# Two-layer cross attention on one core: bias sums added by GpSimd instead of by transfers, and the last layer's vectors loaded later

## The chip, the cores and the metric

The kernel runs on one core of a Trainium2 chip, in fp32 throughout. The metric is the time of one execution on the device, in microseconds (us). The time given for a kernel is the median of its runs; the profile is one further execution.

## What is computed

There are two cross-attention layers over the same context. B = 8 batches of T = 100 query rows of width E = 1024, and per batch S = 1444 context rows of width L = 512.

```python
# layer 0: x is (8, 100, 1024), ctx is (8, 1444, 512)
Q = x @ Wq + bq;  K = ctx @ Wk + bk;  V = ctx @ Wv + bv
w = softmax(Q @ K.T / sqrt(1024), axis=-1)        # over the context rows
x = x + (w @ V) @ Wo + bo
# layer 1: its own weights, the same ctx
q = x @ Wq1 + bq1;  k = ctx @ Wk1 + bk1;  v = ctx @ Wv1 + bv1
w = softmax(q @ k.T / sqrt(1024), axis=1)         # over the query rows
y = w @ v + x
out = (y - mean(y)) * rsqrt(var(y) + 1e-6) * gamma + beta     # mean and variance over the last axis
```

## The kernel before

**Stages.** The kernel never forms keys and values. It first multiplies weights with weights: `qk0` (Wq Wkᵀ of layer 0), then `vo0` (Wv Wo), then, after layer 0's queries, `qk1` (Wq1 Wk1ᵀ). Each of these `weight_products` (L350) is a product in Strassen-Winograd form: seven half-sized products x, z, w, y and so on, issued by `half_steps` (matmul in L166), with the sums of blocks between them on VectorE. Queries then meet the context directly: `scores_by_keys` (matmul in L957) makes the scores of one batch out of `cT` tiles (the context, transposed), and `weighted_rows` (matmul in L910) weighs the `c` tiles (the context as it is) with them. `alternated` interleaves the two: the weighing of batch b with the scores of batch b+2. Then come the output projection of layer 0, the queries of layer 1, and layer 1's attention for the batches 0 to 3, 4 to 6 and 7, with a projection behind each set. `finish` (`untransposed` and `normalise`) ends a batch of layer 1 some batches later; `project_last` ends batch 7.

**Sums for the biases.** A bias turns into weighted sums over the rows of weights, eight scaled 128x1024 rows for each. `transferred_sum` (L549) makes such a sum without VectorE: `scaled_sum` (L580) lets ScalarE write eight scaled copies (L583) and then adds them pairwise, as a tree of seven additions. Each addition is `transfer_added` (L577): a DMA issued by GpSimd from SBUF to SBUF that accumulates into its destination. `key_bias_sums` (L628) does the same for three of the eight terms of `kb0` (128x800 each), and leaves five to VectorE. For `qk1` the tree covers all eight rows (`acc_c`), and for the narrower `acc_u` it adds 128x512 rows.

**Buffers.** Streamed data lies in a pool `stream` of ten "unit" buffers (`unit`); three more buffers of the tag `prob` (`feature_block`) hold `cT` tiles, and in the weight products the scaled rows of the sums. Each batch of each layer loads four `c` tiles, two `cT` tiles into units and two into `prob` buffers, 5.9 MB in all. A `cT` tile is loaded in two parts (L867), in the kernel before as in the changed one.

**Order.** TensorE's order is written out by hand. The loads are issued by SyncE (SP) in a fixed order (`loaded_in_order`, L859, issue in L860), VectorE has stretches in program order (`vector.in_order`), and ScalarE's scaling is in program order; the rest is placed by the scheduler. GpSimd also issues all DMAs of `nc.gpsimd.dma_start`.

**Vectors and output.** After the queries of layer 1 (L1378 to L1388) two units are taken for `vectors` and kept until the end: they hold `gamma`, `beta` and the two halves of `bv1`, each broadcast to 128 partitions. Then `out[0]` to `out[6]` are set to `beta` by seven DMAs of 400 KB from SBUF (L1386), since `normalise` ends with a DMA that accumulates the scaled rows into `out[b]` (L1244). Last, `wv1` is loaded (L1388). `vectors` are first read by `untransposed(0)` in batch 4 of layer 1 (L1229).

## Time and profile before

| | |
|---|---|
| runs, us | 592.06, 594.5, 2132.2 (median 594.5) |
| profiled execution, us | 591.46 |
| its span, us | 589.7 (1.8 us lie around it) |
| TensorE clock granted | 0.996 |
| PE (TensorE matmul) busy, us | 574.6 (97%), 7470 instructions |
| DVE (VectorE) busy, us | 399.9 (68%) |
| POOL (GpSimd) busy, us | 134.7 (23%) |
| ACT (ScalarE) busy, us | 133.2 (23%) |
| DMA | 142.95 MB, mean 242 GB/s; queue q1 (loads) 56.5%, q0 (issued by GpSimd) 19.0% of 16 engines |

How to read the views: the page gives busy times by engine and, in 40 slices of 14.7 us each, the busy share of each engine and of the DMA engines in tenths. The chain is the work that ended last, followed back through what released it. The waits list for each engine and line what it waited for: us in total, times, longest. A table of windows gives for each stretch of time the busy time of PE, PEld (weight load), DVE, ACT and POOL with the count of instructions, the clock, the DMA share (1.00 is all 16 engines busy) and GB/s.

### The profile page before, as it was taken

How to read it: one execution, taken by the hardware profiler on the slowest of the kernel's cores; microseconds unless marked ns; L12 is line 12 of the kernel's file. 1: busy time of each engine (PE TensorE's matmuls, PEld its weight loads, DVE VectorE, ACT ScalarE, POOL GpSimd, SP SyncE). 2: the span in 40 equal slices, each digit the busy share in tenths (PEclk: the TensorE clock that was granted, in tenths of full speed). 3: DMA queues.
4: the chain of work that ended last, by engine and by line, in shares of the span. 5: the costliest groups of instructions: out<-in, count | busy, mean ns of one | idle time of the engine just before them, and what ended most of it. 6: DMA issues, size and time to landing. Idle time of an engine off the chain costs nothing.

```text
span 589.7 us, 17503 instructions
## 1 busy us (share of the span) xinstructions
PE 574.6 (97%) x7470; PEld 496.8 (84%) x7470; DVE 399.9 (68%) x936; ACT 133.2 (23%) x349; POOL 134.7 (23%) x206
## 2 busy tenths in 40 slices
PE   9999999999999999999999999999989999999994
PEld 8887457678899999999998666788989999999992
DVE  1997589879676973956658696957334446754695
ACT  1331421523510112221101001103233302153313
POOL 3110110221211222441123002206622112341052
PEclk9999999999999999999999999999999999999998
DMA  8959989944699999999953507629999991699114
GB/s 277 311 126 319 305 223 285 254 84 100 111 278 344 372 366 363 370 373 359 333 194 100 203 0 300 196 69 375 375 309 316 352 364 46 180 319 281 53 30 83
DMA packets 65096, 142.95 MB, mean 242 GB/s; under 512 B 7548, under 2 KB 12924, under 8 KB 65020
## 3 DMA queue, kind: packets, MB, share of 16 engines
q1 hardware_dynamic: 56574, 117.80, 56.5%
q0 software_dynamic: 8048, 23.57, 19.0%
q8 instruction: 59, 0.97, 0.7%
q10 hardware_dynamic: 398, 0.47, 0.2%
q14 instruction: 17, 0.14, 0.1%
HBM read 121.53 MB, written 6.14 MB: 217 GB/s over the span
## 4 chain that ended last, share of the span: by engine, by line
PE 94%; issue 2%; POOL 1%; DVE 1%; ACT 1%; DVEq 0%; POOLq 0%
PE s L957 22%; PE A L910 21%; PE qk_x L166 7%; PE g_x L166 5%; PE o_x L166 5%; PE vo_x L166 4%; PE o_y L166 3%; PE g_y L166 3%; PE qk_y L166 2%; PE qk_z L166 2%; PE o_z L166 1%; PE o_w L166 1%; PE qk_w L166 1%; PE vo_y L166 1%; PE vo_z L166 1%
## 5 line engine op out<-in xcount | busy, mean ns | idle before, releaser
L910 PE MATMUL A<-w,c 128*64 128x100 f32 (+1 forms) x3072 | 228.5, 249 | 2.7 <-issue 2.7
L910 PEld LDWEIGHTS A<-w,c 128*64 128x64 f32 (+1 forms) x3072 | 202.5, 137 | 3.8 <-issue 3.5
L957 PE MATMUL s<-g1T,cT 128*64 128x100 f32 (+1 forms) x1472 | 114.8, 249 | 3.4 <-issue 3.4
L957 PE MATMUL s<-g0T,cT 128*64 128x100 f32 (+1 forms) x1472 | 112.2, 249 | 0.3 <-issue 0.2
L957 PEld LDWEIGHTS s<-g1T,cT 128*64 128x64 f32 (+1 forms) x1472 | 99.8, 136 | 5.9 <-issue 5.3
L957 PEld LDWEIGHTS s<-g0T,cT 128*64 128x64 f32 (+1 forms) x1472 | 98.8, 136 | 2.9 <-DMA c<-in_ctx 1.3
L1169 POOL TENSOR_TENSOR part<-w 128x500 f32<-128x500 f32 x16 | 26.5, 1655 | 122.5 <-ACT w L1017 58.2
L1149 ACT ACTIVATE w<-w,negmax 128x100 f32<-128x100 f32 x96 | 35.0, 367 | 72.8 <-DVE negmax L99 72.8
L99 DVE SCALAR_TENSOR_TENSOR w<-s,kb 128x400 f32<-128x400 f32 (+2 forms) x32 | 13.9, 464 | 41.1 <-PE s L957 40.9
L1017 ACT ACTIVATE w<-w 128x400 f32<-128x400 f32 (+2 forms) x32 | 12.0, 443 | 120.5 <-DVE w L99 120.5
L99 DVE TENSOR_REDUCE most<-s 128x100 f32<-128x400 f32 (+1 forms) x24 | 12.5, 521 | 36.6 <-PE s L957 36.5
L166 PE MATMUL qk_x<-qk 128*128 128x256 f32 x128 | 29.9, 382 | 0.0
L166 PEld LDWEIGHTS qk_x<-qk 128*128 128x128 f32 x128 | 23.6, 192 | 3.0 <-ACT qk L440 0.2
L1229 DVE SCALAR_TENSOR_TENSOR z<-vectors,r,z 100x512 f32<-100x512 f32 x16 | 11.4, 744 | 12.9 <-PE z L1227 12.8
L99 DVE TENSOR_TENSOR w<-w,rtotal 128x400 f32<-128x400 f32 (+2 forms) x32 | 18.3, 571 | 1.1
L969 POOL MEMSET w<- 68x100 f32 x16 | 3.8, 238 | 64.0 <-PE A L910 46.0
L1242 ACT ACTIVATE z<-z,rstd 100x1024 f32<-100x1024 f32 x7 | 8.0, 1150 | 45.4 <-POOL rstd L1240 45.4
L1149 ACT ACTIVATION_READ_ACCUMULATOR w<-w,negmax 128x1 f32 x96 | 18.1, 188 | 0.0
L99 DVE TENSOR_TENSOR xT<-xT,o_x 128x400 f32<-128x400 f32 (+1 forms) x32 | 15.9, 540 | 2.7 <-PE o_x L166 2.4
L578 POOL DMA_DIRECT2D qk_L_xattn_bk<-qk_L_xattn_bk x6 | 5.2, 922 | 47.3 <-DMA qk_L_xattn_bk<-qk_L_xattn_bk 19.0
L673 ACT ACTIVATE g1T<-g_x,k 128x400 f32<-128x400 f32 x4 | 2.4, 594 | 59.4 <-PE g_x L166 59.3
L166 PE MATMUL vo_x<-vo 128*128 128x512 f32 x32 | 15.3, 595 | 0.0
(435 smaller groups left out, 1052.9 us busy)
## 6 DMA issues: line engine op xcount, KB each, us to landing
c<-in_ctx SPq DMA_DIRECT2D x176, 256.0 KB, 6.1
cT<-in_ctxT SPq DMA_DIRECT2D x64, 370.0 KB, 6.8
cT<-in_ctxT SPq DMA_DIRECT2D x64, 352.0 KB, 5.9
vo<-in_L_xattn_Wo SPq DMA_DIRECT2D x8, 512.0 KB, 7.4
qk<-in_L_xattn_WqT SPq DMA_DIRECT2D x8, 512.0 KB, 6.0
qk<-in_L_xattn_WqT SPq DMA_DIRECT2D x15, 256.0 KB, 4.9
xT<-in_xT SPq DMA_DIRECT2D x2, 1600.0 KB, 24.6
qk_L_xattn_bk<-qk_L_xattn_bk POOLq DMA_DIRECT2D x6, 512.0 KB, 8.5
```

Source lines behind the costliest of these rows:

```text
L99: ins = getattr(nc.vector, op)(*args, **kw)
L166: nc.tensor.matmul(banks[n // per][:, n % per * width : (n % per + 1) * width], lhs[i][:, n * P : (n + 1) * P], rhs[i], start=(fresh and i ...
L578: nc.gpsimd.dma_start(out=to, in_=t, accum_op=ALU.add)
L673: nc.scalar.activation(dst[g][:, c, :], banks[j][:, :GT], AF.Identity, bias=u[:, c : c + 1])
L910: nc.tensor.matmul(ps[h * HP : (h + 1) * HP, k * T : (k + 1) * T], c[m // CQ][:r, m % CQ, k * P + h * HP : k * P + (h + 1) * HP], w[:r, m, :],
L957: nc.tensor.matmul(to, cT[k][:, o : o + n], q[:, k, t0 : t0 + T], start=(k == 0 and m % GM == 0), stop=(k == LC - 1 or (k == LC - 2 and no ...
L969: nc.gpsimd.memset(s["w"][:PAD, MC - 1, :], 0.0)
L1017: nc.scalar.activation(rows, rows, AF.Exp)
L1149: nc.scalar.activation(rows[:, i, :], rows[:, i, :], AF.Exp, bias=negmax[:, i : i + 1], accum_out=total[:, i : i + 1])
L1169: add(part, w[:, 0:5, :], w[:, 5:10, :], ALU.add)
L1229: nc.vector.scalar_tensor_tensor(z[:, half], bv1[j][:T], s["r"], ps[:T, :], ALU.mult, ALU.add)
L1242: nc.scalar.activation(z, z, AF.Copy, scale=rstd)
```

## The change

Two sums no longer use transfers: the seven additions of `acc_c` in `qk1` and the three of `kb0` become `tensor_tensor` instructions of GpSimd (128x1024 and 128x800). The sums of `qk0`, `vo0` and the additions of `acc_u` stay as they are. The two `vectors` units are allocated and loaded behind layer 1's fourth batch (b == 3) instead of ahead of its first. The seven DMAs that set `out[b]` to `beta` no longer read the SBUF tile, but read `beta` from DRAM, broadcast to T rows. The words that came with the change also speak of feature blocks in two parts; the diff has nothing on that.

```diff
-        scaled_sum(tiles[:n], srcs[:n])
+        scaled_sum(tiles[:n], srcs[:n], gpsimd_added if of == "qk1" else transfer_added)
...
+    def gpsimd_added(to, t):
+        nc.gpsimd.tensor_tensor(to, to, t, ALU.add)
+
-    def scaled_sum(tiles, srcs):
+    def scaled_sum(tiles, srcs, added=transfer_added):
...
-                transfer_added(tiles[i], tiles[i + k])
+                added(tiles[i], tiles[i + k])
...
-                scaled_sum(tiles, [(xT[:, k, :], wqbk[:, k : k + 1]) for k in range(EC)])
+                scaled_sum(tiles, [(xT[:, k, :], wqbk[:, k : k + 1]) for k in range(EC)], gpsimd_added)
...
-                transfer_added(to, tiles[0])
+                gpsimd_added(to, tiles[0])
...
-    vectors = [unit(f"vectors_{j}") for j in range(2)]
-    gamma, beta = (t[:, :E] for t in vectors)
-    bv1 = [t[:, E:] for t in vectors]
-    for name, t in (("gamma", gamma), ("beta", beta)):
-        nc.gpsimd.dma_start(out=t, in_=a[f"L1_xattn_{name}"].partition_broadcast(P))
-    for j, t in enumerate(bv1):
-        nc.gpsimd.dma_start(out=t, in_=a["L1_xattn_bv"][j * 512 : (j + 1) * 512].partition_broadcast(P))
     for b in range(B - 1):
-        nc.gpsimd.dma_start(out=out[b], in_=beta[:T])
+        nc.gpsimd.dma_start(out=out[b], in_=a["L1_xattn_beta"].partition_broadcast(T))
...
             if b == 1:
                 AS = project1_sums(wv1)
+            if b == 3:
+                vectors = [unit(f"vectors_{j}") for j in range(2)]
+                gamma, beta = (v[:, :E] for v in vectors)
+                bv1 = [v[:, E:] for v in vectors]
+                for name, v in (("gamma", gamma), ("beta", beta)):
+                    nc.gpsimd.dma_start(out=v, in_=a[f"L1_xattn_{name}"].partition_broadcast(P))
+                for j, v in enumerate(bv1):
+                    nc.gpsimd.dma_start(out=v, in_=a["L1_xattn_bv"][j * 512 : (j + 1) * 512].partition_broadcast(P))
```

## The prediction

> **What bounds the kernel now.** I read the page's shares and slices first, then the chain, TensorE's waits, the tables of windows, and last the transfers around each edit.

> ```profile
> PE 574.6 (97%) x7470; PEld 496.8 (84%) x7470; DVE 399.9 (68%) x936; ACT 133.2 (23%) x349; POOL 134.7 (23%) x206
> ...
> DMA  8959989944699999999953507629999991699114
> ...
> PE 94%; issue 2%; POOL 1%; DVE 1%; ACT 1%; DVEq 0%; POOLq 0%
> ```
> ```profile
> PE s L957 <- issue: 3.5, 6, 1.2
> PE A L910 <- issue: 2.7, 4, 1.1
> PE warm L111 <- DVE ones L108: 1.1, 1, 1.1
> ```

> TensorE is the bound: 574.6 us of a span of 589.7. Its waits are only 7.3 us in all: 1.1 at the very start, and ten gaps before L957 and L910. One of these, 1.15 us at 208.4 us, starts within 0.1 us of the landing of the last tile loaded for its batch, so it is a wait for data. The other nine each follow by about 1.3 us an instruction-fetch packet of 16 KB that took about 1.0 us, in stretches where the DMA engines are full (249 to 265, 420 to 450, 523 to 533 us). So an edit can take away at most 6.2 us, 1% of the time; faster by 2% is out of reach. An edit can lose far more: whatever makes TensorE wait adds in full, since nothing behind it has slack to give back.

> Where could it wait? The start has both other resources full:

> ```profile
> 8.00:10.00 2.00, 2.00 (x11) 1.75 (x10) 0.17 (x1) 0.00 (x0) 0.00 (x0) 1.00 0.96 285
> ...
> 14.00:16.00 2.00, 2.00 (x11) 1.77 (x10) 2.00 (x7) 0.00 (x0) 0.00 (x0) 1.00 0.85 270
> 16.00:18.00 2.00, 2.00 (x12) 1.74 (x10) 2.00 (x7) 0.00 (x0) 0.00 (x0) 1.00 0.94 320
> 18.00:20.00 2.00, 2.00 (x11) 1.77 (x10) 2.00 (x4) 0.00 (x0) 0.00 (x0) 1.00 0.95 283
> ...
> 28.00:30.00 2.00, 2.00 (x11) 1.77 (x10) 2.00 (x4) 0.00 (x0) 0.00 (x0) 1.00 1.06 209
> 30.00:32.00 2.00, 2.00 (x11) 1.77 (x10) 2.00 (x4) 0.20 (x1) 0.00 (x0) 1.00 0.49 96
> ```
> ```profile
> DVE qk_s L99 <- DMA qk<-in_L_xattn_WkT: 5.4, 1, 5.4
> ```

> The last two columns are DMA share and GB/s: the DMA engines have no room from 2 to 30 us. DVE waits for the second halves of WkT until 13.8 us and then works without a gap to 41 us; its T4 blocks are ready at 18.9, while TensorE needs the first of them at 18.64 for `qk_w`. Loads land 1.6 to 3.6 us ahead of TensorE's use (units 4 to 7: 2.2, 3, 3.2, 3.6; first block of A22: 1.6).

> [...]from 358 to 364 us q0's 4096 B packets and q1's of 2816 and 2960 B alternate nearly one for one, at some 142 to 162 and 110 ns each. [...]a GpSimd add of 128x500 that takes 1.25 to 1.34 us alone took 6.02 at 244.5 us beside 16 such DVE instructions in a row, and DVE's `w<-w,rtotal` rose from 0.57 to 1.06 us beside GpSimd's adds at 404 us. [...]the trace's 1.27 to 1.41 us for 128x512 gives 2.5. [...]

> **The change, part by part.** The compiled orders of PE, DVE, ACT and SP are the same in both kernels. Only GpSimd's differs, in three ways.

> (a) *The seven `out` transfers move to the start of the program.* They read no tile any more, so nothing holds them: in GpSimd's order they stand right behind its first memset and the loads of the bias columns. Issue begins at about 5.7 us; five of them also wait for these columns' transfers to finish (landed 5.6 to 8.1 us). Before, they ran here:

> ```profile
> L1386 POOL DMA_DIRECT2D out<-vectors x7: 531/542/577, 368.5 to 371.7; - x7
> ...
> DMA to landing us min/median/max: 3.2/6.7/9.0
> ```

> The trace has 49 packets of 4096 B for each of 15 DMA engines, of about 160 ns (150 to 174): 49 x 0.16 = 7.8 us of engine time. At 370 to 379 us this cost TensorE nothing. At 6 us it shares full engines with the first weight loads, whose packets of 1 and 2 KB take 45 to 100 ns. One packet each in turn gives `out` 160 of some 160 + 90 ns, 64%, so all of it is through after 7.8 / 0.64 = 12 us, by about 19 us; every load that lands after that is late by the whole 7.8 us. WkT's second halves then land at 13.8 + 7.8 = 21.6 instead of 13.8, T4 is ready at 26.7, and `qk_w` starts at about 26.4 instead of 18.64. `qk_z` starts late by some 4 us on the way (its first load has 2.2 us of slack), within the same delay, not on top. From there DVE and TensorE run as before, later by 7.8. Nothing takes it back: TensorE is the bound to the end. Before has no DRAM-to-DRAM transfer, so the packet's cost is bounded: from below by the 110 ns of q1's packets alongside, with part of it caught by the slack of about 2 us (49 x 0.11 - 2 = 3.4 us); from above by accumulating packets of the same 4096 B, which [...]take 300 to 340 ns (49 x 0.3 = 14.7 us). I take 7.8, since source and destination are passed once each as before. Issuing occupies GpSimd for 7 x 0.54 = 3.8 us; its next work, at 23 us, doesn't feel that.

> (b) *Ten additions go from transfers to GpSimd.* An accumulating 512 KB transfer has 8 packets of 4096 B on each engine, in the trace at 300 to 340 ns: about 2.5 us of all 16 engines; a 400 KB one 2. Removed: 7 x 2.5 + 3 x 2 = 23.5 us of DMA time between 140 and 195 us, most of it where the engines are full:

> ```profile
> 150.00:165.00 15.00, 15.00 (x75) 13.32 (x74) 10.01 (x24) 9.88 (x12) 3.99 (x6) 1.00 0.72 142
> 165.00:180.00 15.00, 15.00 (x109) 14.23 (x108) 11.74 (x34) 1.12 (x3) 1.62 (x3) 1.00 1.04 313
> 180.00:195.00 15.00, 15.00 (x280) 14.14 (x280) 9.43 (x24) 0.00 (x0) 1.22 (x3) 1.00 1.06 327
> ```

> Loads are backed up there (one issued at 174.9 landed at 185.6), so the stream of loads comes ahead by several us, and the gap at 208.4 goes: -1.15, perhaps also 0.6 at 264.3. Next in line behind that gap are the fetch gaps, which remain. Added: 7 x 2.5 + 3 x 2.0 = 23.5 us of GpSimd time, beside DVE chains of two SBUF inputs (157.4 to 163.4 without a gap). Either GpSimd waits for them, or an add holds DVE once for up to 2.5 us. Slack: S2 is ready about 5 us ahead of TensorE, the inner blocks of w 3.5, but those of q only 0.9 to 1.1 (ready 179.5, needed 180.4). Bounds: 0 if GpSimd yields, 2.5 - 1 = 1.5 us for one hold at the tight place, 3 for two; I take 0.5. The sum itself should be complete by 180 to 190 us; it is read at 200.9. The `prob` tiles that SP waits for (159.9 and 163.1 before) may come free up to 6 us later, but SP waits for TensorE's release of units until 167 to 171 directly behind, so at most a few us of load issue are lost against 23.5 gained.

> (c) *`vectors` move to b == 3.* From 356 to about 455 us two more of ten units serve the stream. There DMA runs at 0.94 to 1.03 and TensorE loses only to fetches, so I count 0 (bounds -1 and 0). Their 1.5 MB broadcast move into a full stretch, 457 to 470, costing the loads about 1.5 / 0.35 = 4.3 us; `project1` covers it, since the share falls to 0.57 and 0.24 from 480 to 510 us. Without that cover it would be up to 4 us. They are first read at 501.9. I count +0.3.

> (d) Feature blocks are in two parts in both kernels: 0.

> Sum against the profiled 591.46: +7.8 + 0.5 - 1.15 + 0 + 0.3 = +7.4, and I round the relief at 264 in with -0.3: **598.6 us**. The median of the runs shown, 594.5, lies 3 us above the profiled execution; against it the forecast is 0.7% slower.

> **The rivals.**
> 1. *Forecast*, 598.6 (chance 0.52); its own range 594 to 602.
> 2. *The start is not hurt, the freed DMA time pays* (other side, not slower). Place: 6 to 19 us. If two queues' packets overlap on an engine (shares of 1.06 to 1.08 from 26 to 30 us hint at some), or the `out` packets yield to the loads, T4 stays within its slack, and only (b) and (c) count: 591.46 - 1.15 - 0.6 = 589.7. It decides once the delay of WkT's second halves is under 1 us. Against it: the one-for-one alternation seen at 358 us. Chance 0.16.
> 3. *DRAM-to-DRAM packets cost like accumulating ones*: 591.46 + 14.7 - 0.4 = 605.8, with `qk_w` at about 33 us. For it: reading and writing the same memory may be slower than from SBUF; against: the size is passed only once. Chance 0.20.
> 4. *GpSimd's adds hold DVE in `qk1`* at several places, 3 us more of TensorE's gaps between 158 and 185 us: 601.6. For it: DVE is 9 to 12 us of 15 busy there. Against: slack of 3.5 to 5 us at all but one place. Chance 0.12.

> **How the numbers follow.** Cases 1 and 4 lie within 592 to 603, case 2 just under 591 and case 3 up to 608. Low end 591 takes in the low bound of (a), 591.46 + 3.4 - 1.75 - 1 = 592.1, and half of case 2; the high end 608 takes in 14.7 + 3 - 1. Two per cent, about what a measurement of this kernel can tell from no change, is 12 us: 603.4 from the profiled time, 606.4 from the median. So slower comes from most of case 3 (0.15) and the tails of 1 and 4 (0.04): 0.19. Faster by 2% would need 580, under the 583 of a TensorE that waits for nothing: 0.01. Within: 0.80.

> **What would show it.** Right: `out` transfers at 6 to 20 us with packets near 160 ns, DVE's first long wait ending near 21 us, TensorE gaps before `qk_z` and `qk_w` summing to 7 to 8 us, `qk1`'s end 7 us later and no further shift behind it; the gap at 208 (now 216) gone; ten GpSimd adds of 2 to 3 us, longer where they meet DVE. Wrong: `qk_w` still at 19 us (case 2), at 33 (case 3), gaps in L166 between 160 and 190 (case 4), a shift that grows between 455 and 510 us (then (c) was mis-sized), or later work that catches up with the start's delay.

## The result, and the profile after

The changed kernel takes 617.0 us (median of 612.75 to 617.56) against 595.5 for the kernel before in the same comparison: a ratio of 1.0366, 95% interval 1.029 to 1.0442. The ratio is of means and leaves out one run of the kernel before, of 2132.2 us. In the larger sets of runs taken with the experiments, before has a median of 592.2 to 593.6, so the loss is 22 to 25 us. The forecast was 598.6 with a range up to 608. The profiled execution has a span of 614.8 us against 589.7: 25.1 more.

First the page after, the lines that answer to those shown of before (shares, DMA slices, chain):

```profile
PE 583.0 (95%) x7470; PEld 501.0 (81%) x7470; DVE 416.7 (68%) x936; ACT 133.3 (22%) x349; POOL 154.1 (25%) x206
...
PE   8699999999948999999999999999999999999995
...
PEclk9699999999987999999999999999999999999998
DMA  8796998973023899999997401306999993399214
...
PE 87%; DMA 4%; DVE 4%; issue 2%; POOL 1%; ACT 1%; SPq 0%; DVEq 0%; POOLq 0%
```

TensorE runs the same 7470 instructions, but is busy 8.4 us longer, and the chain now holds 4% DMA and 4% DVE. The PE line has two holes, in the second slice (15 to 31 us) and in slices 12 and 13 (169 to 200 us), and the clock line dips in the same places. TensorE's waits name both:

```profile
PE qk_w_x L166 <- DVE qk L99: 9.6, 1, 9.6
PE qk_z L166 <- DMA qk<-in_L_xattn_WkT: 5.3, 3, 3.2
...
PE qk_w L166 <- DVE qk_t L99: 2.4, 1, 2.4
```

Put beside before, product by product, TensorE's lag is 12.9 us where `qk_w` starts (31.55 instead of 18.64), 13.0 at its end and the same until `qk1`. There it is 22.7 at the first `qk_w_x` (186.22 instead of 163.52) and 25.0 at the product `kb` behind it (207.88 instead of 182.93); from there it moves between 23.0 and 25.5 and ends at 25.3. Nothing else in the program adds for good, and nothing gives back. (In the eight kernels whose start is that of before, `qk_w` begins between 18.3 and 19.6 us, so a lag read from one profile is good to about 1 us.)

**The start.** The table of windows of the changed kernel (PE, PEld, DVE, ACT, POOL, clock, DMA share, GB/s):

```profile
8.00:10.00 2.00, 2.00 (x11) 1.77 (x10) 0.17 (x1) 0.00 (x0) 1.60 (x3) 1.00 0.96 262
...
14.00:16.00 2.00, 0.31 (x2) 0.00 (x0) 0.00 (x0) 0.00 (x0) 0.00 (x0) 1.00 0.87 250
...
20.00:22.00 2.00, 1.29 (x4) 0.48 (x2) 0.00 (x0) 0.00 (x0) 0.00 (x0) 0.50 0.78 246
...
26.00:28.00 2.00, 1.38 (x6) 0.77 (x5) 0.00 (x0) 0.00 (x0) 0.00 (x0) 0.78 0.43 146
```
```profile
L1382 POOL DMA_DIRECT2D out<-in_L_xattn_beta x7: 537/544/582, 5.7 to 9.4; - x7
...
DMA to landing us min/median/max: 10.5/15.2/18.7
```
```profile
DVE qk_s L99 <- DMA qk<-in_L_xattn_WkT: 19.4, 1, 19.4
```

The `out` transfers go out at 5.7 to 9.4 us, as forecast, and take turns with the loads (from 10 to 22 us 543 of their packets start and 652 of the loads', of 1 and 2 KB). DVE waits 19.4 us for WkT's second halves instead of 5.4 and starts at 28.3 instead of 13.8. The DMA share is the surprise: instead of 0.85 to 1.08 it falls to 0.8 and then to 0.43.

**The second place.** VectorE and GpSimd between 166 and 186 us, in the view of the timeline (start, length, engine, operation):

```profile
172.50 11.09 DVE L99 TENSOR_TENSOR qk<-qk 128x512 f32<-128x512 f32 x4
183.51 2.89 DVE L99 TENSOR_TENSOR qk<-qk,qk 128x256 f32<-128x256 f32 x2
```
```profile
172.11 2.68 POOL L581 TENSOR_TENSOR qk_L_xattn_bk<-qk_L_xattn_bk,qk_L_xattn_bk 128x1024 f32<-128x1024 f32 x1
174.75 2.80 POOL L581 TENSOR_TENSOR qk_L_xattn_bk<-qk_L_xattn_bk,prob 128x1024 f32<-128x1024 f32 x1
177.51 5.53 POOL L581 TENSOR_TENSOR qk_L_xattn_bk<-qk_L_xattn_bk,qk_L_xattn_bk 128x1024 f32<-128x1024 f32 x2
```

Four DVE instructions of 128x512, which took 0.69 us each before, take 2.8 us each, the length of one GpSimd add. In the same time GpSimd does four adds. Here the two engines alternate: one VectorE instruction for each GpSimd add.

### The profile page after: what moved, and what is told of

The parts are those of the page before. It is cut to its first block, busy times and chain, and to the rows that moved or that the text cites. A ratio compares the mean times of both kernels' runs of the same rounds, so it can differ in the third digit from the quotient of the medians.

```text
span 614.8 us, 17487 instructions
## 1 busy us (share of the span) xinstructions
PE 583.0 (95%) x7470; PEld 501.0 (81%) x7470; DVE 416.7 (68%) x936; ACT 133.3 (22%) x349; POOL 154.1 (25%) x206
## 4 chain that ended last, share of the span: by engine, by line
PE 87%; DMA 4%; DVE 4%; issue 2%; POOL 1%; ACT 1%; SPq 0%; DVEq 0%; POOLq 0%
PE s L960 21%; PE A L913 21%; PE g_x L166 5%; PE o_x L166 5%; PE qk_x L166 5%; DMA qk<-in_L_xattn_WkT 4%; PE vo_x L166 3%; PE o_y L166 3%; PE g_y L166 3%; DVE qk L99 2%; PE qk_y L166 2%; PE o_w L166 1%; PE o_z L166 1%; PE qk_w L166 1%; PE qk_z L166 1%
## 5 line engine op out<-in xcount | busy, mean ns | idle before, releaser
L960 PEld LDWEIGHTS s<-g0T,cT 128*64 128x64 f32 (+1 forms) x1472 | 96.8, 136 | 1.7 <-issue 1.1
L99 DVE SCALAR_TENSOR_TENSOR w<-s,kb 128x400 f32<-128x400 f32 (+2 forms) x32 | 13.9, 463 | 41.2 <-PE s L960 40.9
L99 DVE TENSOR_REDUCE most<-s 128x100 f32<-128x400 f32 (+1 forms) x24 | 12.5, 521 | 36.9 <-PE s L960 36.9
L166 PE MATMUL qk_x<-qk 128*128 128x256 f32 x128 | 31.5, 396 | 0.0
L166 PEld LDWEIGHTS qk_x<-qk 128*128 128x128 f32 x128 | 24.6, 201 | 3.4 <-ACT qk L440 0.2
L166 PE MATMUL qk_z<-qk 128*128 128x256 f32 x64 | 18.5, 448 | 5.3 <-DMA qk<-in_L_xattn_WkT 5.3
L166 PEld LDWEIGHTS qk_z<-qk 128*128 128x128 f32 x64 | 14.1, 225 | 9.4 <-issue 5.8
L99 DVE TENSOR_TENSOR qk<-qk 128x256 f32<-128x256 f32 (+2 forms) x24 | 21.7, 930 | 0.0
L1232 DVE SCALAR_TENSOR_TENSOR z<-vectors,r,z 100x512 f32<-100x512 f32 x16 | 11.4, 742 | 12.8 <-PE z L1230 12.7
L99 DVE TENSOR_TENSOR w<-w,rtotal 128x400 f32<-128x400 f32 (+2 forms) x32 | 18.3, 573 | 1.1
L99 DVE TENSOR_TENSOR xT<-xT,o_x 128x400 f32<-128x400 f32 (+1 forms) x32 | 15.9, 539 | 2.8 <-PE o_x L166 2.4
L185 POOL TENSOR_TENSOR wv_s<-wv 128x512 f32<-128x512 f32 x4 | 5.4, 1356 | 48.5 <-PE g_y L166 48.5
## 6 DMA issues: line engine op xcount, KB each, us to landing
xT<-in_xT SPq DMA_DIRECT2D x2, 1600.0 KB, 24.3
```

The source lines that it names most:

```text
L99: ins = getattr(nc.vector, op)(*args, **kw)
L166: nc.tensor.matmul(banks[n // per][:, n % per * width : (n % per + 1) * width], lhs[i][:, n * P : (n + 1) * P], rhs[i], start=(fresh and i ...
L185: engine.tensor_tensor(t, p, q, op)
L960: nc.tensor.matmul(to, cT[k][:, o : o + n], q[:, k, t0 : t0 + T], start=(k == 0 and m % GM == 0), stop=(k == LC - 1 or (k == LC - 2 and no ...
L1232: nc.vector.scalar_tensor_tensor(z[:, half], bv1[j][:T], s["r"], ps[:T, :], ALU.mult, ALU.add)
```

## Experiments

The first theory after the result: two separate losses, one at the start and one in `qk1`, that add up. Four kernels do one part of the change alone, on the kernel before.

**Only the early `out` transfers** (`out_early`):

```diff
-        nc.gpsimd.dma_start(out=out[b], in_=beta[:T])
+        nc.gpsimd.dma_start(out=out[b], in_=a["L1_xattn_beta"].partition_broadcast(T))
```

> The kernel before with one edit: out[0..6] are set from beta in DRAM, so the seven transfers move to the start of the program; sums and vectors as before. Theory A (the cost of the change is the sum of two separate places, the start and qk1): qk_w starts at about 31.5 us as in the changed kernel, the clock falls to half between 16 and 28 us, and the time is 13 us above before, about 606. Rival B (the start's delay is mostly taken back later, and qk1's additions cost nearly all): under 5 us, below 598. Rival C (all of the loss comes from the start, qk1's gap is a consequence of it): about 616.

Measured: 605.0 us against 592.7; ratio 1.0219 (1.0161 to 1.0276), +12.3 us. `qk_w` starts at 30.6 us.

```profile
PE qk_z L166 <- DMA qk<-in_L_xattn_WkT: 7.1, 2, 5.1
...
PE qk_w L166 <- DMA qk<-in_L_xattn_WqT: 1.2, 1, 1.2
```

This part alone makes half of the loss, all of it before 40 us: `qk_w` starts 11.9 us late, runs in part at half the clock (granted 0.50 from 24.3 to 34.6 us), and `qk_y` behind it starts 14.0 us late.

**Only `qk1`'s additions by GpSimd** (`adds_qk1`):

```diff
-        scaled_sum(tiles[:n], srcs[:n])
+        scaled_sum(tiles[:n], srcs[:n], gpsimd_added if of == "qk1" else transfer_added)
```

> The kernel before with one edit: the seven additions of acc_c in qk1 by GpSimd; kb0 and out as before. Theory A (each GpSimd add holds off one VectorE instruction with two SBUF inputs for its whole length, and TensorE waits at qk_w_x): a gap of 9 to 10 us ahead of qk_w_x, a clock near 0.5 for some 5 us behind it, +12 us, less 1 us for the freed DMA time: about 604. Rival D (kb0's three additions, which make VectorE late by 4 us just ahead, are half of it): a gap of 4 to 6 us, +6, about 598. Rival C (a consequence of the start): 592 or less.

Measured: 603.5 against 592.7; 1.0188 (1.0129 to 1.0247), +10.8 us, with the start and `kb0` as before. TensorE's wait and VectorE's instructions in this stretch:

```profile
PE qk_w_x L166 <- DVE qk L99: 10.1, 2, 8.9
```
```profile
L99 DVE TENSOR_TENSOR qk<-qk x4: 2822/2835/2857, 159.4 to 167.7; 128x512 f32<-128x512 f32 x4
L99 DVE TENSOR_TENSOR qk_s<-qk_s,qk x2: 691/1390/2090, 155.6 to 157.4; 128x512 f32<-128x512 f32 x2
L99 DVE TENSOR_TENSOR qk<-qk,qk x2: 2554/2559/2564, 170.4 to 172.9; 128x256 f32<-128x256 f32 x2
```

Seven instructions, one for each add, are stretched to 2.1 to 2.9 us, those of 0.4 us (128x256) as much as those of 0.7: what counts here is the length of the add (2.4 to 2.8 us for the seven in the changed kernel). It is no consequence of the start, nor of `kb0`.

**Only `kb0`'s additions** (`adds_kb0`; the two edits of `key_bias_sums` in the diff):

> The kernel before with one edit: the three additions of kb0 (128x800) by GpSimd. Theory A: two or three VectorE instructions are stretched from 0.7 and 1.0 to about 2.5 us, which TensorE's slack of some 5 us ahead of S2 and w hides: 0 to +1 us, 592 to 595. Rival D (kb0's additions are half of the loss at qk1): +4 to +6, about 598.

Measured: 593.3 against 592.7; 0.9988 (0.9963 to 1.0012). Two VectorE instructions are stretched to 2.7 and 2.4 us here as well, but TensorE waits for neither: the only wait for VectorE in its list is the 1.1 us at the very start, and no gap appears in `qk1`.

**Only the late vectors** (`vectors_late`; `out` set from the tile directly behind):

```diff
+                for n in range(B - 1):
+                    nc.gpsimd.dma_start(out=out[n], in_=beta[:T])
```

> The kernel before with one edit: vectors loaded behind layer 1's fourth batch, and out[0..6] set from the SBUF tile of beta right behind that load; sums as before. Theory A: nothing is won by two more units, since the DMA engines are full there, and the 4.4 MB of transfers at 457 to 480 us hide under project1: within 1 us of before, 592 to 595. Rival E (the late transfers delay the loads of the next batches): gaps of TensorE between 480 and 520 us, +3 us or more.

Measured: 594.2 against 592.7; 1.0032 (1.0014 to 1.0051), a small but real loss. Its profile has TensorE gaps of 0.9, 0.8 and 0.8 us at 464, 471 and 477 us, where before has none between 450 and 520. That doesn't show where the loss arises: each of the three follows an instruction-fetch packet, as the gaps of before do (59 such packets of 16 KB there, of about 1.0 us each); `adds_kb0`, which leaves the vectors early, has gaps of 0.6, 1.2, 0.2 and 0.6 us between 460 and 487 us; and all gaps of this kind sum to 6.7 us here and 6.2 in before. A gap where the rival expected it, between 480 and 520 us, isn't there.

The sum of the parts is 12.3 + 10.8 + 1.5 = 24.6 us, with `kb0` at nothing; 617.0 - 592.7 is 24.3. By the ratios the four parts make 4.3%, the whole 3.7% (2.9 to 4.4). So the parts add up within what these runs can tell.

**The changed kernel without the early transfers** (`after_out_late`: `out` set from `beta`'s tile behind the late load, as in the last diff):

> The changed kernel with one part undone: out[0..6] are set from the SBUF tile of beta behind the late load of vectors, so nothing but weights is loaded at the start. If the losses of the parts add up (12.3 for the start, 10.8 for qk1's additions, 1.5 for the late vectors): qk_w at 18.6 us again, and 592.7 + 10.8 + 1.5 = 605. If the start's delay made qk1's worse, or kb0's additions ahead of qk1's do: 600 or 609.

Measured: 603.8 against 593.2; 1.017 (1.0113 to 1.0228). `qk_w` is back near its old place (the lag there is 0.9 us), the wait at `qk_w_x` is 9.6 us again. The start's delay and `kb0`'s additions do not make it worse.

**Shorter adds** (`adds_qk1_quarters`):

```diff
+        for n in range(4):
+            part = slice(n * E // 4, (n + 1) * E // 4)
+            nc.gpsimd.tensor_tensor(to[:, part], to[:, part], t[:, part], ALU.add)
```

> The kernel before with qk1's seven additions by GpSimd, each cut into four of 128x256. If each add lets one VectorE instruction with two SBUF inputs through and holds the next off for its own length (0.7 us instead of 2.7): VectorE has its 13 instructions ahead of qk_w_x done about 9 us late instead of 15, TensorE's gap there is 3 to 5 us instead of 10, and the time about 598. If the sum of the adds' lengths counts (19 us, however cut): 603 as with whole rows.

Measured: 599.3 against 593.2; 1.009 (1.006 to 1.0121), +6.1 us. TensorE waits 4.0 us at `qk_w_x`. The profiled run is 3.7 us above that median, so only its durations are read here. VectorE's same four instructions, and GpSimd's adds beside them:

```profile
157.40 4.63 DVE L99 TENSOR_TENSOR qk<-qk 128x512 f32<-128x512 f32 x4
```
```profile
156.88 6.61 POOL L583 TENSOR_TENSOR qk_L_xattn_bk<-qk_L_xattn_bk,prob 128x256 f32<-128x256 f32 x6
```

Four in 4.6 us instead of 11.1, each beside an add of 1.1 to 1.2 us. The alternation holds at the finer grain: VectorE gets one instruction through per add, and a shorter add holds it off for less. The work is not hidden, it only blocks less at a time.

**TensorE kept at work in the wait** (`adds_qk1_warm`):

```diff
+            for _ in range(32 if name == "qk1_w" else 0):
+                nc.tensor.matmul(X[:, :P], ones, ones, start=True, stop=True)
```

> The kernel before with qk1's seven additions by GpSimd, and 32 matmuls of ones (7.6 us at full clock, into the bank that qk_w_x then starts afresh) that TensorE does while it waits for VectorE. If the clock that falls in the 9 us wait costs 2 to 3 us beside the wait itself: no slow matmuls behind, about 601. If the clock costs nothing: 603.5 as without them; if they delay qk_w_x: more.

Measured: 601.3 against 593.6; 1.0115 (1.0079 to 1.0151). The interval overlaps that of `adds_qk1`, so the whole time alone does not settle it; the windows do. First `adds_qk1`, then this kernel, the same five microseconds (the second is ahead, so the matmuls are not the same ones):

```profile
175.00:180.00 5.00, 4.49 (x17) 4.13 (x18) 4.35 (x15) 0.37 (x1) 0.41 (x3) 0.50 0.02 3
```
```profile
175.00:180.00 5.00, 5.00 (x36) 4.72 (x35) 5.00 (x19) 0.74 (x2) 0.00 (x0) 1.00 0.11 15
```

At a clock of 0.50 TensorE does 17 matmuls, at 1.00 it does 36. The lag at the first scores behind `qk1` is 13.9 us in the one and 11.3 in the other: with 0.2 us between their starts taken off, some 2.5 us of the loss in `qk1` is the slow clock behind the wait, not the wait. The account closes within a microsecond: 10.1 us of wait and 2.5 of slow clock, less the 1.4 that the next experiment gives for the freed transfers, are 11.2 us against the 10.8 of `adds_qk1`.

**What the freed DMA time is worth** (`qk1_not_added`):

```diff
+    def not_added(to, t):
+        pass
...
+        scaled_sum(tiles[:n], srcs[:n], not_added if of == "qk1" else transfer_added)
```

> The kernel before with the seven additions of acc_c in qk1 left out altogether (the sum is then not that of the eight rows), by transfer or by GpSimd: what taking 7 x 512 KB of transfers out of 155 to 195 us is worth by itself, with no cost against it. If the load stream there limits TensorE: the gap at 208 us goes and the time is 1 to 2 us under before, 591. If those gaps come from something else: no difference, 592.7.

Measured: 591.6 against 593.2; 0.9977 (0.9954 to 0.9999). Taking the seven transfers away at no cost brings 1.4 us by the ratio, hardly clear of nothing and by the interval 2.7 at most. So no way of adding these rows could have won much.

**The source of the early transfers** (`out_early_sbuf`):

```diff
+    start = row("start")
+    nc.vector.memset(start, 0.0)
+    for b in range(B - 1):
+        nc.gpsimd.dma_start(out=out[b], in_=start[:T])
```

> The kernel before with the seven transfers to out[0..6] at the start of the program, but out of an SBUF tile that VectorE sets to zero (beta's value in the inputs) instead of out of beta in DRAM: the same 700 packets of 4096 B to the same place. If sharing the DMA engines packet by packet is what costs: the loads as late as with DRAM as the source, qk_w at 30 us, about 605. If DRAM to DRAM is the costly part (its packets slower, its engines finishing up to 6 us apart): qk_w at about 26 us as first forecast, +7 to +8, about 600.

Measured: 601.9 against 593.2; 1.015 (1.0094 to 1.0205), `qk_w` at 28.2 us. Between the two expectations, and not a clean comparison: these transfers were issued from 2.4 us on, 3.3 us earlier than in `out_early`, and already held up `qk_x`. The packets tell more: 4096 B from SBUF or from DRAM have a median of 159 ns alike, with a mean of 211 here, 241 in `out_early` and 184 in the changed kernel (205 in before at 370 us). The means from DRAM lie on both sides of that from SBUF, so the source isn't shown to be what made the transfers dear; whether it adds a few microseconds stays open.

**Three of seven early** (`out_three_early`: `in_=beta[:T] if b > 2 else` the broadcast from DRAM):

> The kernel before with three of the seven out transfers at the start (out of beta in DRAM) and four where they were. If the loss is in proportion to the packets that take their turns with the loads: 3/7 of 12.3, so +5.3, about 598. If the loads' lead of some 2 us and DVE's wait absorb a short burst and only a long one starves SP's eight loads in flight: +2 or less, 595.

Measured: 598.3 against 593.6; 1.0078 (1.0047 to 1.0109), +4.6 us; `qk_w` is 5.1 us late. The loss is about proportional to the packets (3/7 of 12.3 is 5.3): no slack absorbs a part of them.

**The same transfers in the loads' own queue** (`out_sp_behind`):

```diff
             for h in [H + i for i in range(H)] + list(range(H)):
                 nc.sync.dma_start(out=units[h][:, lh:l_width], in_=lsrc[:, h, lh:])
+            for n in range(B - 1):
+                nc.sync.dma_start(out=out[n], in_=a["L1_xattn_beta"].partition_broadcast(T))
```

> The kernel before with all seven out transfers early and out of beta in DRAM, but issued by SP, in its order directly behind the last load of qk0 and ahead of vo0's. The same packets in the same crowded stretch, only in the loads' own queue. If taking turns with qk0's loads is what costs: qk_w starts at 18.6 us, vo0's loads come 8 to 12 us later, which TensorE needs only from 44 us on: 0 to +2, 593 to 595. If the bytes cost wherever they stand before 30 us: +8, 601.

Measured: 593.6 against 593.6; 1.0002 (0.9982 to 1.0022). The same 2.9 MB from DRAM to DRAM, still in a stretch where the engines are full (a share of 0.97 to 1.08 from 20 to 30 us in before), cost nothing that the times show when they stand behind `qk0`'s loads in one queue. Their packets pass from 21 us on instead of from 9:

```profile
DVE qk_s L99 <- DMA qk<-in_L_xattn_WkT: 5.2, 1, 5.2
```

DVE's wait is 5.2 us, as before. So the loss at the start is not the bytes as such but that they take turns with loads which somebody waits for. The queue and the time changed together here: whether GpSimd's own queue would be as harmless if it issued as late was not run. TensorE falls back by 0.5 us at `vo_z`, whose loads now come behind them.

**The change with both parts mended** (`after_mended`: the changed kernel, `out` by SP as above, `qk1`'s additions by transfers):

> The changed kernel with its two costly parts mended: out[0..6] set by SP directly behind qk0's loads, and qk1's additions by transfers again; kb0's additions by GpSimd and the late vectors stay. If the two parts are the whole loss and the 1.5 us of the late vectors came from the 2.9 MB of out transfers behind them: 593, within 0.2% of before. If the late load of vectors itself costs: 595. If something else of the change costs as well: more.

Measured: 596.9 against 592.2; 1.0073 (1.0046 to 1.0099), so it is the last case, more than 595. Its profiled run, the fastest of its eleven, shows one place for certain: at `vo_z`, which waits for vo0's loads, TensorE falls back by 1.8 us, so the `out` transfers by SP are not quite free. At the late load of `vectors`, with no `out` transfers near it, TensorE has gaps of 0.7, 1.6 and 0.8 us between 464 and 479 us, each again behind an instruction-fetch packet:

```profile
PE A L915 <- issue: 3.0, 4, 1.6
PE vo_z L166 <- DMA vo<-in_L_xattn_Wo: 1.1, 2, 0.7
```

That the late vectors cost by themselves, without `out` behind them, fits both kernels that have them; one trace each doesn't show it. This profile's span is 2.7 us above that of before, the medians are 4.7 apart; the rest stays open. No version that was run and computes the same result beats the kernel before.

## Why the prediction was wrong

- **The bound and the ceiling on a gain** held: TensorE's work is unchanged, and leaving seven transfers out altogether brought 1.4 us (0.1 to 2.7), against 1.15 to 1.75 expected. That the gap at 208.4 us is a wait for data, as the prediction reads it, is not settled: it ends 1.6 us behind an instruction-fetch packet of 1.03 us, much as the other nine do.
- **Step (a), the start, was right in its mechanism and mis-sized: 7.8 us forecast, 12.3 measured alone.** `qk_w` is 11.9 us late in `out_early` and 12.9 in the changed kernel. The place, the issue at 5.7 us, the turns with the loads' packets and the chain from WkT over VectorE's sums to `qk_w` are as predicted (in `out_early` a load of WqT ends `qk_w`'s wait in place of the sums). The term that failed is the length of a turn. The prediction took 160 + 90 = 250 ns for one `out` packet and one packet of the loads, so that the `out` work is through after 12 us. From 10 to 22 us the 16 engines passed 543 `out` packets in the changed kernel and 547 in `out_early`, one per engine every 354 and 351 ns, and the `out` work lasted 18 us, from 9 to 27. Where the prediction had seen the turns, in before at 361 to 364 us, 176 and 178 packets passed: 273 ns a turn, about the sum of their own 159 and 117. At the start, by 28 us, the loads were 13.4 and 12.8 us behind those of before (by the bytes moved in their queue). Before, the changed kernel and `out_early`, in this order:

```profile
10.00:22.00 12.00, 12.00 (x57) 10.56 (x56) 8.22 (x20) 2.15 (x3) 0.00 (x0) 1.00 0.96 321
```
```profile
10.00:22.00 12.00, 8.07 (x28) 5.98 (x27) 0.00 (x0) 1.17 (x2) 0.00 (x0) 0.78 0.83 264
```
```profile
10.00:22.00 12.00, 8.42 (x38) 6.77 (x37) 0.00 (x0) 1.17 (x2) 0.00 (x0) 1.00 1.01 260
```

So the rate fell alike, from 321 to 264 and 260 GB/s, but not in the same way: in the changed kernel the `out` packets have a mean of 184 ns and the engines stand idle for a sixth of the time, in `out_early` the engines stay full and the mean is 241 ns. The median is 159 in both, which the prediction took for all packets; the mean of the `out` packets in before was already 205. In both traces the engines finish one load at very different times: in the changed kernel a load issued at 7.9 us is finished by its first engine at 18.9 us and by its last at 25.5, and SP, with eight loads in flight, issued the next only when one was complete on all engines (15.8, 17.4, 19.6, 22.7 us). Why a turn took 350 ns stays open; no run tested it.
- **Step (b), the additions, failed: 0.5 us taken, 3 as the upper bound, 10.8 measured.** The prediction was right that a GpSimd add can hold up VectorE, as `w<-w,rtotal` at 404 us showed (1.06 us instead of 0.57), and reckoned with one or two holds of 2.5 us. The runs show a hold for every add: seven adds in a row stretch seven VectorE instructions by some 14 us in sum, of which 3.5 us of slack ahead of w take the first part and TensorE waits for the rest (10.1 us). Looking at slack place by place was the error: VectorE ran these instructions one behind another without a gap (168.1 to 190.3 us in the changed kernel), so each hold is added to the last. The trace of before had a case in which GpSimd did the yielding (the add of 6.02 us), and I gave it too much weight. At 404 us, from where the prediction quotes one stretched instruction, it was the first of three, one for each of GpSimd's first three adds there (first VectorE, then GpSimd, in before):

```profile
404.00 1.06 DVE L99 TENSOR_TENSOR w<-w,rtotal 128x400 f32<-128x400 f32 x1
...
405.18 1.34 DVE L99 TENSOR_TENSOR w<-w,rtotal 128x300 f32<-128x300 f32 x1
...
406.63 1.15 DVE L99 TENSOR_TENSOR w<-w,rtotal 36x100 f32<-36x100 f32 x1
```
```profile
403.36 2.83 POOL L185 TENSOR_TENSOR wv_s<-wv 128x512 f32<-128x512 f32 x2 [31.12 <-PE g_y L166]
406.16 2.75 POOL L185 TENSOR_TENSOR wv_s<-wv_s,wv 128x512 f32<-128x512 f32 x2
```

- **A term was missing.** The prediction put the clock at nothing. In `adds_qk1` TensorE began to wait at 164.2 us, for 8.9 us in one piece; the granted clock fell to 0.50 at 166.6 and stayed there until 180.3, some 7 us beyond that piece's end. This cost 2.5 us in `qk1`, and 2.1 in `out_early`, where `qk_w` took 9.0 us instead of 6.9. In the changed kernel the half clock of the start (16.7 to 26.9 us) fell into time that TensorE waited through anyway.
- **Step (c), late vectors:** +0.3 taken, +1.5 measured between medians (1.9 by the ratio). Where it arises is not shown.
- **The rivals.** Rival 4 was the right mechanism at a third of its price, rival 1 the right mechanism at two thirds. Rival 3 gave 605.8, close to the 605.0 of `out_early`, by luck: it took 300 ns for every packet, while the median is 159 and the mean 184 to 241, and it had no slow clock. The top of the range, 608, did let the dear start and rival 4 come true together; it fell short because rival 4's 3 us were 10.8.

## What to carry to other kernels

Ask where a DMA goes when its source is made independent of the program. Here the seven `out` DMAs moved to the program's start (5.7 us), into the one stretch where everybody waits for loads, took turns with them from another queue and cost 12.3 us; tie such DMAs behind the loads in the loads' own queue, where these cost nothing that the times show (593.6 us against 593.6). Before handing additions to GpSimd, count VectorE's instructions with two SBUF inputs in the same stretch: in a row of adds each held back one of them for about its full length here (2.1 to 2.9 us), so many long adds beside a chain in order were the worst case (+10.8 us) and short ones a lesser evil (+6.1). When TensorE is the bound, price a wait of several us as its length and the slow clock behind it (10.1 and 2.5 us in `adds_qk1`; a wait of 3.5 us in `adds_qk1_warm` left the clock at 1.00). And read a gap of under 1 us from more than one profile: here such gaps wandered between kernels that do the same thing at that place.
